# A row of numbers behind every gather of layers 1 and 2

## The chip, the cores and the metric

The kernel runs on one core of a Trainium2 chip. The metric is the device time of one execution in microseconds (us). Before the change three runs took 1017.23, 1017.79 and 1019.32 us; the median is 1017.79 us. The engines are TensorE (PE in the profile; PEld is its weight load), VectorE (DVE), ScalarE (ACT), GpSimd (POOL) and SyncE (SP), beside 16 DMA engines.

## The reference, cut to what matters

The reference puts four graph layers over a node matrix `x` of 2708 x 512 floats and one adjacency matrix `adj` of 2708 x 2708, which is sparse and has its largest degrees in the first rows. Each layer is wrapped as `x = layernorm(x + layer(x, adj))`.

```python
# layer 1
head = mask / maximum(sqrt(sum(mask * mask, -1)), EPS)   # mask = adj > 0
inc = adj + head
y = (inc @ x) / sum(inc, -1)
# layer 2
type_sum = adj @ x
attn_a = sigmoid(concat(type_sum, x) @ Wa.T + ba)         # attn_b likewise with Wb, bb
h = x @ W_sa
e = where(adj != 0, exp(-leaky_relu(s_left[:, None] + s_right[None, :], 0.01)), 0)
x_a = (e / (sum(e, 1) + 1e-5)) @ h
x_b = adj @ (x @ W_gcnb) + b_gcnb
y = sigmoid(attn_a * x_a + attn_b * x_b)
```

Layer 0 is a normalised `adj @ x` followed by a projection, and layer 3 multiplies the adjacency with the product of the signs of `x` and of a weight. Layers 1 and 2 are the ones that the change touches.

## The kernel before

**Blocks and tiles.** The 2708 rows are 22 blocks of up to 128 rows (`NB`, the last has 20 rows). Column block 0 of the adjacency is dense enough to be kept whole; for every other block `b` the kernel finds the nodes that have an edge into it, and packs their adjacency rows into `ROOM[b]` tiles of 128 nodes each (`packed[b]`, lists of node numbers in `index[b]`). `ROOM` falls from 9 to 4, and is 1 for the last block; over all blocks that makes 107 tiles. A tile that is used by only 64 of the block's rows is multiplied as a half tile (`HALVES`).

**A first stage** reads the adjacency, makes the lists, projects `x` for layer 0, and fetches the packed rows with one indirect DMA for each tile (`fetch`, L1011). Behind each of those fetches, for the groups in `RESTED` (L1008: all groups but the last three), GpSimd also fills a scratch tile `rest` of 128x384 floats with zeros (L1018).

**Gathers.** Each of the layers then gathers, for every one of its tiles, the feature rows of that tile's 128 nodes from a DRAM copy, with one indirect DMA that GpSimd issues: `gathered` (L582) for layers 0, 1 and 3, `gathered_2` (L1719) for layer 2. In layer 1 a row is 512 floats (256 KB a gather), in layer 2 it is 1026 floats, the features, their projection `h` and two scores (about 525 KB).

**Layer 1** (L1507 to L1615) goes over the blocks in the order 0, 1, 21, 2, 3, ... (`sequence`). For a block it issues all gathers (L1581 to L1583), lets DVE make the incidence tiles (`inc`, L1597, L1598), and PE adds the products of all tiles into one PSUM bank (`add_tile`, L1316). Between the blocks PE also transposes and projects the finished block before (`project1`, L1526 and L1533, with ACT copies at L1528 and L1539) and adds to block 0's sums for layer 2 (`grow2`, L1566 and L1567). The gathers have eight buffers: the pool `s_l1` has `bufs=8`. A gather can start when the tile eight places earlier has been multiplied.

**Layer 2** (L1621 to L1907) does the parts of a block in turn. For each part, `prepare` issues the gathers, and ACT and DVE make the attention weights: a score is added by ACT for each tile (L1489), DVE applies the slope (L1490), a mask (L1492, L1493), and ACT the exponential (L1494). `accumulate` then multiplies each tile twice, once with weights and once with the adjacency (L1744). Here the gathers have seven buffers. The layernorm of this layer has one small power operation on GpSimd for each block (L644), which sits in the same queue as the gathers.

**Order.** Each engine runs its instructions in one fixed order. In the first stage the text's order is forced (`in_order`); elsewhere the framework's scheduler chooses it at build time, from priorities in the order of the text and from its own model of durations and readiness. A dependency without a semaphore (`NoSync`) only constrains that order.

Of the kernel before, what the change touches and what calls it, by code (L numbers as in the profile page):

```python
# [19 lines left out]
P = 128  # L20
# [475 lines left out]
def sparse_layers(ctx, tc, x, adj, adj_t, w0_t, b0, w_sa, a_sa, w_gcnb, b_gcnb, wa, ba, wb, bb, w3_t,  # L496
# [11 lines left out]
    nc = tc.nc  # L508
# [7 lines left out]
    def rows(b: int) -> int:  # L516
        return min(P, N - b * P)

    def direct(b: int):

        return tuple(range(NB)) if b == 0 else DIRECT.get(b, ())
# [4 lines left out]
    const = ctx.enter_context(tc.tile_pool(name="s_const", bufs=1))  # L526
# [46 lines left out]
    dia_pos = const.tile([P, NB], F32, name="s_dia_pos")  # L573
    own0 = const.tile([P, NB], F32, name="s_own0")
    own1 = const.tile([P, NB], F32, name="s_own1")
    head0_row = const.tile([P, P], F32, name="s_head0_row")
    cols = const.tile([P, NB, EXTRA], F32, name="s_cols")

# [3 lines left out]
    def gathered(pool, dst_w: int, src, b: int, i: int, dtype=F32):  # L582
        t = pool.tile([P, dst_w], dtype, tag="xg", name=f"xg{b}_{i}")
        nc.gpsimd.indirect_dma_start(  # L584
            out=t, out_offset=None, in_=src[:, :],
            in_offset=bass.IndirectOffsetOnAxis(ap=index[b][:, i : i + 1], axis=0),
        )
        return t

    @contextmanager  # L590
    def in_order():
# [77 lines left out]
    with tc.tile_pool(name="s_pre", bufs=1) as pre:  # L669
# [36 lines left out]
        for d in (y_rows, x1_rows, x2_rows, xw_rows):  # L706
# [17 lines left out]
            channel_multiplier=-1,  # L724
# [5 lines left out]
            base=-1, channel_multiplier=-1,  # L730
# [5 lines left out]
            base=1 - P, channel_multiplier=1,  # L736
# [540 lines left out]
    def features(b: int, i: int, old0):  # L1277

        j = direct(b)[i]
        return f[j] if j else old0  # L1280
# [196 lines left out]
    def open_sums(b: int):  # L1477

        k = banks[0] % 2
        banks[0] += 1  # L1480
        state[b]["sums"] = [
            ps_acc.tile([P, D], F32, tag=f"{c}{k}", name=f"{c}{b}") for c in ("e", "a")
        ]

    def weights_of(e, mask, parts):

        for ev, _, sl, _, scores in parts:
            for i, score in enumerate(scores):
                nc.scalar.activation(ev[:, i, :], sl, AF.Identity, bias=score)  # L1489
        nc.vector.scalar_tensor_tensor(e, e, SLOPE, e, op0=ALU.mult, op1=ALU.max)  # L1490
        for _, mv, _, a, _ in parts:
            nc.vector.tensor_scalar(mv, a, 0.0, MASKED, op0=ALU.is_equal, op1=ALU.mult)  # L1492
        nc.vector.tensor_tensor(e, e, mask, op=ALU.add)  # L1493
        nc.scalar.activation(e, e, AF.Exp, scale=-1.0)  # L1494
# [12 lines left out]
    with tc.tile_pool(name="s_l1", bufs=8, reuse_waits="tile") as lp:  # L1507
        def gate_columns(dst, c: int, pool, tag: str):

            pv = pool.tile([P, D], F32, tag=tag, name=f"pv2_{c}")  # L1510
            nc.tensor.transpose(pv[:, : 2 * KC], vrows[:, c, :], ident[: 2 * KC, : 2 * KC])
            nc.vector.tensor_copy(
                dst.rearrange("p k t -> p t k"),
                pv[:, : 2 * KC].rearrange("p (t k) -> p t k", t=2),
            )

        gate_columns(wsa[:, :, D + 2 :], 0, ps_mm, "mm")
        H = D // 2
        hs = {}

        def project1(j: int):

            m = rows(j)
            pt = ps_mm.tile([P, KC, P], F32, tag="sum0", name=f"xt1p_{j}", bufs=1)
            for k in range(KC):
                nc.tensor.transpose(pt[:, k, :m], f[j][:m, k * P : (k + 1) * P], ident[:m, :m])  # L1526
            xt = lp.tile([P, KC, P], F32, tag="xt1", name=f"xt1_{j}", bufs=2)
            nc.scalar.copy(xt[:, :, :m], pt[:, :, :m])  # L1528
            p0 = ps_acc.tile([P, D], F32, tag="a1", name=f"h0_{j}")
            p1 = ps_acc.tile([P, D], F32, tag="e1", name=f"h1_{j}")  # L1530
            for ps, w in ((p0[:m, :H], wsa[:, :, :H]), (p1[:m, : H + EXTRA], wsa[:, :, H:])):
                for k in range(KC):
                    nc.tensor.matmul(  # L1533
                        ps, xt[:, k, :m], w[:, k, :], start=(k == 0), stop=(k == KC - 1)
                    )
            h = kept[j] if j < 2 else lp.tile(
                [P, D + EXTRA], F32, tag="h", name=f"h_{j}", bufs=4
            )
            nc.scalar.copy(h[:m, :H], p0[:m, :H])  # L1539
            nc.vector.tensor_copy(h[:m, H:], p1[:m, : H + EXTRA])  # L1540
            nc.sync.dma_start(x2_rows[j * P : j * P + m, D:], h[:m, : D + 2])
            nc.vector.tensor_copy(cols[:m, j, :], h[:m, D:])
            hs[j] = h

        grown2 = []

        def grow2(js):

            r, n, st = rows(js[0]), len(js), state[0]
            e = lp.tile([P, G2, P], F32, tag="e0", name=f"e0_{js[0]}", bufs=2)[:r, :n, :]  # L1550
            mask = lp.tile([P, G2, P], F32, tag="mask0", name=f"m0_{js[0]}", bufs=1)[:r, :n, :]
            a = packed[0][:r, js[0] : js[0] + n, :]
            weights_of(
                e, mask, [(e, mask, st["sl"][:r], a, [cols[:r, j, 0:1] for j in js])]
            )
            for i in range(n):
                if grown2 or i:
                    nc.vector.tensor_tensor(
                        st["esum"][:r], st["esum"][:r], e[:, i, :], op=ALU.add
                    )  # L1560
                else:
                    nc.vector.tensor_copy(st["esum"], e[:, i, :])
            for i, j in enumerate(js):
                at = dict(start=(not grown2), stop=(len(grown2) == NB - 1))
                se, sa = st["sums"]
                nc.tensor.matmul(se, e[:, i, :], hs.pop(j)[:r, :D], **at)  # L1566
                nc.tensor.matmul(sa, a[:, i, :], f[j][:r], **at)  # L1567
                grown2.append(j)

        G2 = 2  # L1570
        left = [(0, 1), (NB - 1,)] + [
            tuple(range(j, min(j + G2, NB - 1))) for j in range(2, NB - 1, G2)
        ]

        for at, b in enumerate(sequence):
            m = rows(b)
            if b:
                nd = len(direct(b))
                order_ = in_turns(b)
                src = {i: features(b, i, first[1]) for i in range(nd)}  # L1580
                for i in order_:  # L1581
                    if i >= nd:
                        src[i] = gathered(lp, D, x1_rows, b, i - nd)  # L1583
                ps = ps_mm.tile([P, D], F32, tag="mm", name=f"l1_{b}")
                inc_of = {}
                for i0, n, (r0, r1) in runs_of(b, 3):
                    a = packed[b][:, i0 : i0 + n, r0:r1]
                    half = r1 - r0 == HALF
                    inc = lp.tile(
                        [P, 3, HALF if half else P], F32, tag=f"inc{int(half)}",  # L1590
                        name=f"inc{b}_{i0}", bufs=4 if half else 3,
                    )
                    iv = inc[:, :n, : r1 - r0]
                    row = head_row[:, None, b * P + r0 : b * P + r1].to_broadcast(
                        [P, n, r1 - r0]
                    )
                    nc.vector.scalar_tensor_tensor(iv, a, 0.0, row, op0=ALU.is_gt, op1=ALU.mult)  # L1597
                    nc.vector.tensor_tensor(iv, iv, a, op=ALU.add)  # L1598
                    for i in range(n):
                        inc_of[i0 + i] = iv[:, i, :]  # L1600
                for i in order_:
                    add_tile(ps, b, i, inc_of[i], src[i][:, :D], order_)
            else:
                ps = sum1
            if left and left[0][-1] in sequence[: max(at - 2, 0)]:
                grow2(left.pop(0))
            finish1(b, ps)
            if at:
                project1(sequence[at - 1])
            if at == 1:  # L1610
                open_block(0, wp2, ps_mm, "mm")
                open_sums(0)
        project1(sequence[-1])
        for js in left:
            grow2(js)  # L1615
# [5 lines left out]
    with tc.tile_pool(name="s_l2o", bufs=1, reuse_waits="tile") as op, \  # L1621
# [97 lines left out]
        def gathered_2(b: int, t: int):  # L1719
            g = lp.tile([P, XW], F32, tag="xg", name=f"xg2_{b}_{t}", bufs=7)  # L1720
            nc.gpsimd.indirect_dma_start(  # L1721
                out=g, out_offset=None, in_=x2_rows[:, :],
                in_offset=bass.IndirectOffsetOnAxis(ap=index[b][:, t : t + 1], axis=0),
            )
            return g

        def accumulate(b: int, c: int):
# [402 lines left out]
```

## Time and profile before

The profile is of one execution, which was itself slower than the timed runs.

| what | value |
|---|---|
| timed runs, median | 1017.79 us |
| the profiled execution's own time | 1063.61 us |
| its span, first to last instruction | 1061.9 us |
| mean granted PE clock | 0.942 |
| PE busy | 893.4 us (84%) |
| DVE busy | 663.5 us (62%) |
| POOL busy | 569.7 us (54%) |
| ACT busy | 385.5 us (36%) |
| gathers of layer 1, L584 from `x_rows` | 107, 968 ns each |
| gathers of layer 2, L1721 from `x_rows` | 107, 993 ns each |
| layer 1 | about 382 to 622 us |
| layer 2 | about 622 to 934 us |

A line of groups in the profile names a line of the kernel, an engine, an operation and its tiles (output<-inputs), then the count, the busy time in us and the mean duration of one in ns, and then the idle time of the engine just ahead of it with what ended most of it. "remote" is a wait that ended with no instruction that the profile could name as its end; "issue" is a gap for which it shows no wait. The names leave buffer numbers out, so `x_rows` stands for layer 1's and layer 2's DRAM copies alike.

### The profile page before, as it was taken

Reading aid. Unit: us, or ns where it says so; the run is one execution under the profiler, and the core shown is the slowest. Engines: PE = TensorE matmul, PEld = TensorE weight load, DVE = VectorE, ACT = ScalarE, POOL = GpSimd, SP = SyncE. Lnnn points to the kernel's source line nnn. Section 1 sums busy time; section 2 is a strip of 40 time slices with the busy share of each in tenths; the row PEclk is TensorE's granted clock in tenths of the full one; section 3 lists DMA queues with packets and bytes.
Section 4 is the critical chain, followed back from the end, with each engine's and each line's share of the span. In section 5 each row is a group of like instructions: output and inputs, shape, how many; then the busy total and the mean of one; then the engine's idle time right before and its main releaser. Section 6 shows DMA issues by size and latency. Waiting matters only on the chain.

```text
span 1061.9 us, 13166 instructions
## 1 busy us (share of the span) xinstructions
PE 893.4 (84%) x3793; PEld 465.5 (44%) x3793; DVE 663.5 (62%) x2571; ACT 385.5 (36%) x821; POOL 569.7 (54%) x621
## 2 busy tenths in 40 slices
PE   1989996078788978899999999998889999689994
PEld 1545552022123324455455543443535555467772
DVE  4899998125566745345555346666758877646666
ACT  3566662000000013445344334333334333255554
POOL 1799998766666544555434034534434333057762
PEclk9899999589898988999999999999999999989996
DMA  9999984356776745666645266668677665299986
GB/s 265 349 321 322 336 263 144 82 171 209 231 210 207 227 139 145 184 209 189 208 144 168 95 233 216 238 223 288 205 230 230 200 195 201 80 269 311 321 233 214
DMA packets 96294, 231.16 MB, mean 218 GB/s; under 512 B 14204, under 2 KB 27884, under 8 KB 96212
## 3 DMA queue, kind: packets, MB, share of 16 engines
q0 software_dynamic: 46896, 139.22, 44.3%
q1 hardware_dynamic: 37368, 76.25, 20.9%
q10 hardware_dynamic: 11948, 14.76, 4.3%
q8 instruction: 32, 0.52, 0.2%
q14 instruction: 50, 0.41, 0.1%
HBM read 188.51 MB, written 31.71 MB: 207 GB/s over the span
## 4 chain that ended last, share of the span: by engine, by line
PE 52%; DVE 12%; DMA 11%; POOL 10%; another core or an unknown queue 6%; issue 6%; ACT 3%; ACTq 0%; POOLq 0%; SPq 0%; DVEq 0%
PE l L1316 14%; DMA xg<-x_rows,i 8%; PE h L1533 7%; POOL a L1013 6%; PE l L1999 4%; PE a L1744 4%; PE e L1744 4%; PE l L2038 3%; POOL s_rest L1018 3%; PE pg L1796 2%; PE pc L1796 2%; PE l L1371 2%; PE e L1566 1%; PE px L1857 1%
## 5 line engine op out<-in xcount | busy, mean ns | idle before, releaser
L1721 POOL DMA_INDIRECT xg<-x_rows,i x107 | 106.2, 993 | 170.3 <-PE a L1744 40.9
L584 POOL DMA_INDIRECT xg<-x_rows,i x107 | 103.6, 968 | 115.9 <-PE l L1316 73.1
L1013 POOL DMA_INDIRECT a<-in_adj_t_dram,row_at x107 | 115.8, 1082 | 46.6 <-DVE deg L773 21.4
L584 POOL DMA_INDIRECT xg<-y_rows,i x107 | 104.6, 978 | 52.6 <-issue 24.1
L1316 PE MATMUL l<-xg,a 128*64 128x512 f32 (+1 forms) x214 | 98.0, 652 | 27.5 <-DMA xg<-y_rows,i 26.9
L584 POOL DMA_INDIRECT xg<-xw_rows,i x76 | 79.6, 1048 | 38.6 <-issue 17.9
L1744 PE MATMUL a<-xg,a 128*64 128x512 f32 (+1 forms) x214 | 92.8, 603 | 4.5 <-DMA xg<-x_rows,i 4.5
L1744 PE MATMUL e<-xg,ae 128*64 128x512 f32 (+1 forms) x214 | 90.3, 603 | 2.7 <-ACT ae L1494 2.6
L1533 PE MATMUL h<-s_wsa,xt 128*128 128x256 f32 (+3 forms) x352 | 83.8, 392 | 6.9 <-ACT xt L1528 6.8
L1045 PE MATMUL y<-s_w,xt 128*128 128x512 f32 (+1 forms) x176 | 86.9, 640 | 0.0
L1316 PE MATMUL l<-xg,inc 128*64 128x512 f32 (+1 forms) x214 | 79.4, 613 | 3.6 <-DMA xg<-x_rows,i 3.1
L1533 PEld LDWEIGHTS h<-s_wsa,xt 128*128 128x128 f32 (+1 forms) x352 | 65.0, 189 | 33.5 <-ACT xt L1528 15.6
L1489 ACT ACTIVATE ae<-sl,xg 128x64 f32<-128x64 f32 (+1 forms) x107 | 37.5, 359 | 99.1 <-DMA xg<-x_rows,i 88.6
L765 ACT ACTIVATE unused<-arow 128x1408 uint8<-128x1408 f32 (+3 forms) x44 | 58.3, 1325 | 3.8 <-DMA x_rows<-s_zero 3.0
L1316 PEld LDWEIGHTS l<-xg,a 128*64 128x64 f32 (+1 forms) x214 | 25.1, 160 | 78.4 <-DMA xg<-y_rows,i 41.5
L1424 DVE SCALAR_TENSOR_TENSOR t<-l,s_dinv,f 128x512 f32<-128x512 f32 (+1 forms) x21 | 15.6, 744 | 64.6 <-remote 44.7
L1999 PE MATMUL l<-ws,pw 128*128 128x512 f32 (+1 forms) x210 | 51.5, 400 | 3.9 <-DVE pw L1927 3.9
L613 ACT ACTIVATE rsqs<-mv 128x1 f32<-128x1 f32 (+2 forms) x56 | 11.3, 202 | 112.1 <-DVE mv L642 45.8
L1540 DVE COPY h<-h 128x260 f32<-128x260 f32 (+1 forms) x20 | 8.6, 428 | 66.3 <-PE h L1533 47.5
L1045 PEld LDWEIGHTS y<-s_w,xt 128*128 128x128 f32 (+1 forms) x176 | 33.8, 203 | 36.5 <-issue 36.4
L1490 DVE SCALAR_TENSOR_TENSOR ae<-ae 128x128 f32<-128x128 f32 (+5 forms) x56 | 19.2, 343 | 45.8 <-ACT ae L1489 45.1
L1796 PE MATMUL pg<-s_wg,pt 128*128 128x256 f32 (+1 forms) x176 | 44.7, 392 | 2.8 <-ACT pt L1784 2.8
(302 smaller groups left out, 1887.2 us busy)
## 6 DMA issues: line engine op xcount, KB each, us to landing
arow<-in_adj_dram SPq DMA_DIRECT2D x21, 704.0 KB
arow<-in_adj_dram SPq DMA_DIRECT2D x21, 650.0 KB
x_rows<-f SPq DMA_DIRECT2D x41, 256.0 KB
aw<-in_adj_t_dram SPq DMA_DIRECT2D x21, 320.0 KB
f<-in_x_dram SPq DMA_DIRECT2D x20, 256.0 KB
y_rows<-yt ACTq DMA_DIRECT2D x20, 256.0 KB
out_dram<-f SPq DMA_DIRECT2D x20, 256.0 KB
x_rows<-h SPq DMA_DIRECT2D x19, 257.0 KB
```

The source lines that it names most:

```text
L584: nc.gpsimd.indirect_dma_start(out=t, out_offset=None, in_=src[:, :], in_offset=bass.IndirectOffsetOnAxis(ap=index[b][:, i : i + 1], axis=0),)
L765: nc.scalar.activation(unused[:m, : ar.shape[1]], ar, AF.Copy, accum_out=row_sums[:m, b, h : h + 1])
L1013: nc.gpsimd.indirect_dma_start(out=packed[b][:, t + len(direct(b)), :], out_offset=None, in_=adj_t, in_offset=bass.IndirectOffsetOnAxis(ap ...
L1018: nc.gpsimd.memset(rest, 0.0)
L1045: nc.tensor.matmul(ps[:m], xt[:, k, :m], w0[:, k, :], start=(k == 0), stop=(k == KC - 1))
L1316: nc.tensor.matmul(ps[r0:r1], weights, moving, start=(i == order[0]), stop=all(span(b, j) != (r0, r1) for j in order[order.index(i) + 1 :] ...
L1489: nc.scalar.activation(ev[:, i, :], sl, AF.Identity, bias=score)
L1533: nc.tensor.matmul(ps, xt[:, k, :m], w[:, k, :], start=(k == 0), stop=(k == KC - 1))
L1721: nc.gpsimd.indirect_dma_start(out=g, out_offset=None, in_=x2_rows[:, :], in_offset=bass.IndirectOffsetOnAxis(ap=index[b][:, t : t + 1], a ...
L1744: nc.tensor.matmul(ps[r0:r1], weights, moving, start=(i == order[0]), stop=all(span(b, k) != (r0, r1) for k in order[order.index(i) + 1 :] ...
L1796: nc.tensor.matmul(ps, pt[:, k, :m], w[:, k, :], start=(k == 0), stop=(k == KC - 1))
L1999: nc.tensor.matmul(whole[b], p[:r, h, b * P : (b + 1) * P], g[:r, :], start=(j == 0 and h == 0), stop=(j == NB - 1 and h == 1),)
```

## The change

A scratch tile `numbers` of 128x448 16-bit integers is added to the constants. A new helper finds the last instruction that was traced for GpSimd, which is the gather, writes the numbers 0 to 447 into every row of the scratch tile with an `iota` on GpSimd, and ties the iota behind the gather in the build-time order. It is called behind each of the 107 gathers of layer 1 and each of the 107 of layer 2. Nothing reads the scratch tile.

```diff
+    numbers = const.tile([P, 448], mybir.dt.int16, name="s_numbers")
...
+    def last_on_pool():
+        return next(
+            i for i in reversed(nc.cur_bb.bb.instructions) if i.engine == mybir.EngineType.Pool
+        )
+
+    def rest_behind_gather():
+        gather = last_on_pool()
+        nc.gpsimd.iota(numbers, pattern=[[1, 448]], base=0, channel_multiplier=0)
+        tc.add_manual_dep(
+            last_on_pool(), gather.name,
+            mybir.DependencyInfo(mybir.DependencyClass.NoSync, mybir.DependencyReason.DATA),
+            reason="rest_behind_gather",
+        )
...
                 for i in order_:
                     if i >= nd:
                         src[i] = gathered(lp, D, x1_rows, b, i - nd)
+                        rest_behind_gather()
...
                 in_offset=bass.IndirectOffsetOnAxis(ap=index[b][:, t : t + 1], axis=0),
             )
+            rest_behind_gather()
             return g
```

## The prediction

> **What bounds the kernel now.** I read the busy time by stage first (columns: stage in us, its length, busy us and count of PE, PEld, DVE, ACT, POOL, granted PE clock, DMA share, GB/s). The third row is layer 1, the fourth layer 2.
>
> ```profile
> 0.00:177.00 177.00, 141.61 (x1022) 78.25 (x1022) 150.38 (x660) 98.37 (x175) 136.97 (x178) 0.96 0.88 286
> 177.00:382.00 205.00, 141.77 (x425) 43.48 (x424) 105.47 (x462) 11.48 (x43) 130.01 (x132) 0.86 0.63 188
> 382.00:622.00 240.00, 224.21 (x774) 118.53 (x775) 115.00 (x461) 98.02 (x170) 103.87 (x108) 0.96 0.57 168
> 622.00:934.00 312.00, 279.92 (x1152) 142.56 (x1150) 213.68 (x765) 112.75 (x308) 119.27 (x129) 0.99 0.64 211
> ```
>
> PE carries both layers: it idles 15.8 us in layer 1 and 32.1 us in layer 2. POOL is free for 136 and 193 us there, so 107 more instructions in each have room on average; what matters is where they fall. Second, the groups and waits of the engines concerned.
>
> ```profile
> L1721 POOL DMA_INDIRECT xg<-x_rows,i x107 | 106.2, 993 | 170.3 <-PE a L1744 40.9 <-ACT ae L1489 36.5 <-PE e L1744 34.7
> L584 POOL DMA_INDIRECT xg<-x_rows,i x107 | 103.6, 968 | 115.9 <-PE l L1316 73.1 <-issue 22.6 <-DVE inc L1597 15.5
> L1018 POOL MEMSET s_rest<- 128x384 f32 x82 | 44.0, 537 | 0.1
> L743 POOL IOTA s_slot<- 128x1152 int16 x1 | 1.1, 1089 | 0.0
> L750 POOL IOTA s_start_i<- 128x22 int32 x1 | 0.1, 137 | 0.0
> ```
>
> ```profile
> ACT ae L1489 <- DMA xg<-x_rows,i: 88.6, 61, 3.9
> ```
>
> GpSimd mostly waits for PE to free a buffer; in layer 2 ACT in turn waits for gathers to land, 61 times, 88.6 us in all. Third, the timeline of POOL: two rested fetches of the first stage, then the unrested run that opens layer 1.
>
> ```profile
> 150.43 1.00 POOL L1013 DMA_INDIRECT a<-in_adj_t_dram,row_at  x1 [0.16 <-issue]
> 151.43 0.43 POOL L1018 MEMSET s_rest<- 128x384 f32 x1
> 152.03 0.94 POOL L1013 DMA_INDIRECT a<-in_adj_t_dram,row_at  x1 [0.16 <-issue]
> ...
> 390.06 0.95 POOL L584 DMA_INDIRECT xg<-x_rows,i  x1 [0.30 <-issue]
> 391.32 0.95 POOL L584 DMA_INDIRECT xg<-x_rows,i  x1 [0.30 <-issue]
> ```
>
> Unrested gathers follow each other every 1.25 us (0.95 + 0.30 gap), rested ones about every 1.55 to 1.6 (0.95 + 0.43 + 0.16). Fourth, the timeline at the end of that run of 17 gathers, and the clock by stage around it.
>
> ```profile
> 400.22 2.88 PE L1533 MATMUL h<-s_wsa,xt 128*128 128x256 f32 x12
> 406.11 0.37 ACT L1539 COPY s_h<-h 128x256 f32<-128x256 f32 x1 [10.44 <-remote]
> 407.73 0.45 PE L1469 MATMUL slp<-s_ident,s_cols 128*128 128x128 f32 x1 [4.62 <-DVE rs L633]
> ```
>
> ```profile
> 402.00:406.00 4.00, 1.11 (x6) 0.61 (x4) 2.12 (x6) 0.00 (x0) 1.37 (x2) 1.00 0.66 174
> 406.00:413.00 7.00, 5.27 (x10) 2.23 (x11) 4.19 (x17) 2.29 (x6) 0.94 (x1) 0.51 0.35 117
> 438.00:443.00 5.00, 3.89 (x12) 3.12 (x13) 0.00 (x0) 2.39 (x4) 1.89 (x2) 0.72 0.53 153
> ```
>
> The matmuls of `h` show as ended by 403.1, yet ACT's copy, which waits only for them, starts at 406.11: PE's completion was told 3.0 us late, shortly after the gathers paused. PE then waits 4.62 us for what follows from that copy, and runs its next 7 us at clock 0.51. The same recurs after the run from 418 to 437: ACT's L1528 idles 1.96 us for "remote" until 438.47, then PE idles 3.02 us until 439.11. In the trace's record of PE's semaphore, lags of 2 us and more occur in layer 0, layer 1 and layer 3, all during unrested runs of nine or more gathers; none occurs in the rested first stage (at most 1.1 us, at a higher DMA share), nor in layer 2, whose runs have at most nine and mostly four.
>
> **What the Trainium skill says.** SBUF — State Buffer, § Who interferes with whom: VectorE in its two-port mode and a GpSimd instruction lock each other out for a whole instruction; a GpSimd one that only writes does not disturb two-input VectorE work. The trace agrees in that the rest takes 432 ns at least but up to 1079. Perfetto Trace Analysis, § GPSIMD Engine Instruction: time GpSimd by start-to-start spacing; I do so. The same page, § Tensor Engine Instruction: a matmul's end is an estimate. So the 3.0 us lag could be PE still working; but at clock 1.00 twelve matmuls begun 0.22 us apart leave no such backlog. TensorE: Matmul & The Clock Gate, § What's actually happening: about 3.4 us of idling halve the clock; 0.51 after 406 agrees.
>
> **The change part by part.** Nothing is removed.
>
> *The scratch tile* costs nothing by itself; 896 bytes a partition only move addresses.
>
> *Price of one iota.* From the two rows, (1089 - 137) / (1152 - 22) = 0.84 ns an element, so 137 + 426 x 0.84 = 0.50 us (the 22-wide one is 32-bit; if width counted, 448/1152 x 1089 = 0.42). As with the fill, the gap behind it should be 0.16. Back to back, a gather then takes 0.95 + 0.50 + 0.16 = 1.61 us instead of 1.25: +0.36. POOL gets 214 x 0.50 = 107 us of work into 329 us of idle time. Against an idle queue the iota runs while GpSimd waits for a buffer, and costs 0.
>
> *Layer 1, lateness.* Adding 0.36 for each gather in a run, and taking idle time off, the opening run is late by 2.8 us at its ninth gather and 5.3 at its sixteenth. The ninth was used 6.65 us after issue; the first three were used as soon as 3.6 to 4.8 us after theirs. So its margin is 1.8 to 3.0: PE loses 0 to 1.0 us. The sixteenth had 17.9 us: hidden by block 1's projection and block 21. In the run from 418 the gathers at 423.62 and 425.04 have 5.4 and 5.05 us, and come 1.4 and 1.8 late: another 0 to 1.5. Every later one has over 7.4 us except one at 459.06 (5.8, 1.1 late). Together 0 to 2.5; I take 0.8. If PE's other work did not cover it, the opening would pass on all 2.8.
>
> *Layer 1, relief.* If rests stop the late completions as they seem to in the first stage, this returns 3.0 us at 403 and 2.0 at 438, and the half clock behind them: 7 x 0.49 = 3.4 and 5 x 0.28 = 1.4. That is 9.8 us at most, and 0 at least. I take half, 4.9, because the run is only thinned from 1.25 to 1.61 and a part of the lag may belong to the profiled execution.
>
> *Layer 2, gathers.* ACT's adds that wait for landings start at 689.33, 691.34, 693.07 and 694.93, so landings are 1.7 to 2.0 us apart: the 525 KB transfer, not the issue, spaces them. 1.61 is still below. The delay is hidden by the transfer of the gather before, 0; if not, it is the rival below.
>
> *Layer 2, queue.* Behind each iota sit the next gather and the power operations (22 x about 0.58 us). In five places (659.19, 765.53, 779.54, 812.01, 822.60) the power operation directly follows a gather and would start up to 0.5 us later, with DVE's L654 behind it and the gather after it: at most 5 x 0.5 = 2.5, mostly under PE's other products. *VectorE lock.* Iotas fill 53 us of layer 2's 312, 17%. Some 170 two-port operations (78 of L1492, the rest L654, L1844 and the like, eight a block) would be blocked 0.25 us on average in 17% of cases: 7 us of DVE, which is 68% busy; at most a third, 2.4, reaches PE. For both together I take 0.7 of 0 to 4.9.
>
> *Order.* The scheduler sees a longer POOL and may shift instructions on other engines. The trace can't price that; I bound it at -3 to +3 and take 0.
>
> Sum against the profiled execution: -4.9 + 0.8 + 0.7 = -3.4, so 1063.6 becomes 1060.2. That execution lies 45.8 us above the median; I carry the difference over: 1017.8 - 3.4 = 1014.4.
>
> **The rivals.** *Slower: the issue decides layer 2's landings.* Place: ACT's L1489. If transfers alone would land closer than 1.61 us, each of 61 waits grows by 0.36: 22 us for ACT, of which PE's idle share (32.1 of 88.6, 36%) is 7.9. With no relief and layer 1's 0.8: 1026.5; with a third of the waits affected, 1021.2. Against it: the spacing of 1.7 to 2.0. For it: 61 waits with no margin. *No difference.* The late completions stay, or exist only under the profiler, and everything else is hidden, or relief and costs cancel: 1017 to 1019. For it: POOL's idle time; against it: exact balance is a narrow target. *Full relief*: -9.8 + 1.5 = 1009.5. *It doesn't do what it says* (iotas gathered elsewhere in the queue): the tie and the text's order speak against it; time as before.
>
> **How the numbers follow.** A measurement can tell about 0.2%, 2 us, from no change. Relief beats cost: 0.43 (partial 0.31, full 0.12), own range 1008 to 1015.7. No difference: 0.19. Slower: 0.38, for the lateness, the lock and a worse order each have no cover that I can prove. Range 1007 to 1024: 0.08 lie below (full relief with a lucky order), 0.10 above.
>
> **What would show it.** 107 iotas in each layer at about 0.5 us; runs spaced 1.6 us; ACT's L1539 starting close behind PE's last `h` in block 0, no "remote" waits near 406 and 438, clock near 1 there; ACT's wait for landings in layer 2 still near 89 us. I am wrong if those waits stay or move, if ACT's wait grows by ten us or more, or if layer 1 shortens in the profile but not in the timed runs.

## The result, and the profile after

The changed kernel took 1027.97 us (median of 7 runs, 1023.91 to 1032.29) against 1019.32 us for the kernel before in the same runs: a ratio of 1.0081, 95% interval 1.0054 to 1.0107. It is slower by about 8 us; the forecast was 1014.4 us.

The groups of the changed kernel in the page (busy us, mean ns | idle us ahead of it), and its GpSimd in the run that opens layer 1 (start, length, gap ahead):

```profile
L1737 POOL DMA_INDIRECT xg<-x_rows,i x107 | 105.3, 984 | 107.5 <-PE a L1761 34.8
L585 POOL DMA_INDIRECT xg<-x_rows,i x107 | 103.7, 969 | 53.0 <-PE l L1331 24.3
L598 POOL IOTA s_numbers<- 128x448 int16 x214 | 111.4, 521 | 2.1
```

```profile
371.75 0.95 POOL L585 DMA_INDIRECT xg<-x_rows,i  x1 [0.17 <-issue]
372.71 0.52 POOL L598 IOTA s_numbers<- 128x448 int16 x1
373.39 0.95 POOL L585 DMA_INDIRECT xg<-x_rows,i  x1 [0.17 <-issue]
```

The rows do what was foreseen of them: 0.52 us each (forecast 0.50), gathers in a run 1.64 us apart (forecast 1.61). The idle time ahead of the gathers is 53.0 and 107.5 us in layers 1 and 2, against 98.6 and 168.1 us in the second profile of the kernel before (below). (Lines of the changed kernel stand 15 to 17 later: L1316 is L1331, L1489 is L1504, L1721 is L1737, L1744 is L1761.)

By layer, counted here and below from a layer's first gather to the next layer's, the changed kernel shows (length, busy us of PE, PEld, DVE, ACT, POOL, clock, DMA share, GB/s):

```profile
363.20:595.20 232.00, 227.50 (x774) 117.86 (x775) 117.68 (x461) 98.35 (x170) 159.06 (x214) 0.98 0.59 174
595.20:911.20 316.00, 281.47 (x1136) 142.19 (x1152) 222.27 (x766) 113.75 (x308) 174.93 (x236) 0.98 0.64 209
```

Against the profile that the forecast read (239.6 us counted the same way), layer 1 is *shorter* by 7.6 us; so is layer 0, which the change does not touch: its gathers ran from 210.4 to 348.5, and from 210.0 to 366.9 before. The whole span is 31 us shorter, while the timed runs are 8 us longer. The two profiles cannot be subtracted.

### The profile page after: what moved, and what is told of

Read it like the earlier page. It is cut to its first block, busy times and chain, and to the rows that moved or that the text cites. A ratio compares the mean times of both kernels' runs of the same rounds, so it can differ in the third digit from the quotient of the medians.

```text
span 1030.6 us, 13347 instructions
## 1 busy us (share of the span) xinstructions
PE 898.0 (87%) x3775; PEld 463.8 (45%) x3793; DVE 676.8 (66%) x2571; ACT 387.1 (38%) x821; POOL 680.6 (66%) x835
## 3 DMA queue, kind: packets, MB, share of 16 engines
q0 software_dynamic: 46896, 139.22, 45.8%
## 4 chain that ended last, share of the span: by engine, by line
PE 48%; DMA 19%; DVE 13%; POOL 11%; issue 6%; ACT 2%; ACTq 0%; POOLq 0%; SPq 0%; DVEq 0%
PE l L1331 9%; DMA xg<-y_rows,i 9%; DMA xg<-x_rows,i 8%; PE h L1548 6%; PE l L2016 5%; PE a L1761 4%; PE e L1761 4%; PE l L2055 4%; POOL xg L585 3%; PE y L1060 3%; POOL a L1028 3%; POOL s_numbers L598 2%; DVE s_mask L843 2%; PE pc L1813 2%; PE pg L1813 2%
## 5 line engine op out<-in xcount | busy, mean ns | idle before, releaser
L1737 POOL DMA_INDIRECT xg<-x_rows,i x107 | 105.3, 984 | 107.5 <-PE a L1761 34.8
L1028 POOL DMA_INDIRECT a<-in_adj_t_dram,row_at x107 | 112.2, 1048 | 45.8 <-DVE deg L788 20.8
L1331 PE MATMUL l<-xg,a 128*64 128x512 f32 (+1 forms) x214 | 101.3, 625 | 30.1 <-DMA xg<-y_rows,i 28.5
L598 POOL IOTA s_numbers<- 128x448 int16 x214 | 111.4, 521 | 2.1
L585 POOL DMA_INDIRECT xg<-xw_rows,i x76 | 77.3, 1017 | 34.2 <-issue 13.2
L1761 PE MATMUL a<-xg,a 128*64 128x512 f32 (+1 forms) x214 | 92.3, 613 | 5.6 <-DMA xg<-x_rows,i 5.6
L1761 PE MATMUL e<-xg,ae 128*64 128x512 f32 (+1 forms) x214 | 88.5, 613 | 5.8 <-ACT ae L1509 5.8
L1331 PE MATMUL l<-xg,inc 128*64 128x512 f32 (+1 forms) x214 | 83.7, 608 | 2.8 <-DMA xg<-x_rows,i 2.7
L1548 PEld LDWEIGHTS h<-s_wsa,xt 128*128 128x128 f32 (+1 forms) x352 | 64.6, 188 | 28.8 <-ACT xt L1543 10.7
L1504 ACT ACTIVATE ae<-sl,xg 128x64 f32<-128x64 f32 (+1 forms) x107 | 38.0, 359 | 80.7 <-DMA xg<-x_rows,i 72.0
L1331 PEld LDWEIGHTS l<-xg,a 128*64 128x64 f32 (+1 forms) x214 | 24.7, 152 | 86.1 <-DMA xg<-y_rows,i 61.7
L659 POOL TENSOR_TENSOR rs<-mv,s_neg_half 128x1 f32<-128x1 f32 (+1 forms) x22 | 14.0, 635 | 58.5 <-DVE mv L657 56.2
L1033 POOL MEMSET s_rest<- 128x384 f32 x82 | 48.9, 596 | 0.1
```

The costliest lines, as they stand in the source:

```text
L585: nc.gpsimd.indirect_dma_start(out=t, out_offset=None, in_=src[:, :], in_offset=bass.IndirectOffsetOnAxis(ap=index[b][:, i : i + 1], axis=0),)
L598: nc.gpsimd.iota(numbers, pattern=[[1, 448]], base=0, channel_multiplier=0)
L1028: nc.gpsimd.indirect_dma_start(out=packed[b][:, t + len(direct(b)), :], out_offset=None, in_=adj_t, in_offset=bass.IndirectOffsetOnAxis(ap ...
L1033: nc.gpsimd.memset(rest, 0.0)
L1331: nc.tensor.matmul(ps[r0:r1], weights, moving, start=(i == order[0]), stop=all(span(b, j) != (r0, r1) for j in order[order.index(i) + 1 :] ...
L1548: nc.tensor.matmul(ps, xt[:, k, :m], w[:, k, :], start=(k == 0), stop=(k == KC - 1))
```

## The experiments

Two devices recur. The scheduler is shown one width of the number row while it orders the program, and the width is changed afterwards (`set_rests`), so that order and time are separated. With the number rows left out, rows of 4 leave the order of the kernel before on every engine, as far as the names and shapes in the traces tell; rows of 448 give a new one in the opening blocks of layer 1 and in layer 2, mostly blocks 1 to 12. And the gathers of one block can be followed by all its number rows together.

A row need not stand directly behind its gather. The tie only puts it somewhere behind: at 11 of the 107 gathers of layer 2 (14 in the changed kernel) the layernorm's power operation stands between the gather and its row.

The five sessions of experiments were of two kinds. In three of them the kernel before took 1016.35, 1016.75 and 1016.45 us, in two 1068.66 and 1067.8 us. The expectations call this a difference of chips. One chip was used in a session of each kind, so the chip alone does not make it; I say "quick" and "long" sessions.

### The kernel before, profiled again

No edit.

> The kernel before, unchanged, profiled a second time. Theory 'the lag belonged to one execution': the 45.8 us that the first profile lay above the timed runs are gone (a span of about 1020 us), no PE completion near the gather runs of layer 1 arrives late, the first layer (which the change does not touch) is again near 138 us of gathers as after the change, not 157, and layer 1 is shorter than after's 232 us, near 226. Rival 'unrested gathers delay completions': layer 1 again carries some 10 us of waits with the releaser 'remote' or half clock, and lies near 240 us.

It took 1015.18 us with a span of 1013.5 us. Its layers 1 and 2:

```profile
362.80:585.40 222.60, 218.15 (x774) 115.84 (x775) 115.01 (x461) 98.12 (x170) 103.58 (x108) 0.99 0.60 182
585.40:895.40 310.00, 279.02 (x1136) 142.66 (x1153) 214.39 (x766) 112.97 (x309) 119.23 (x130) 0.99 0.64 213
```

The lag is gone: layer 0's gathers end at 347.3, no wait in the whole trace ends with "remote", and block 0's copy of `h` starts at 380.10, 17.3 us after the layer's first gather, not 24.0:

```profile
378.93 2.88 PE L1533 MATMUL h<-s_wsa,xt 128*128 128x256 f32 x12
380.10 0.37 ACT L1539 COPY s_h<-h 128x256 f32<-128x256 f32 x1 [5.51 <-PE h L1533]
```

It starts 1.2 us after the twelve matmuls begin, because L1539 copies the first half of `h` only and needs just the first four of the twelve. So in the first profile, where they began at 400.22, the copy at 406.11 was 4.7 us late, not 3.0. That profile was of a long session's kind; in layer 1 it had, among others,

```profile
ACT s_h L1539 <- remote: 10.4, 1, 10.4
ACT xt L1528 <- remote: 2.0, 1, 2.0
```

Seen against this profile, the changed kernel is 9.4 us longer in layer 1 and 6.0 in layer 2 (6.4 us, and 4.5 and 5.7, in two later executions of it). Such differences scatter by some us: the stages ahead of layer 1, which no edit touches, take 356.6 to 363.2 us in the eleven quick executions. None of the eleven has a wait for "remote": there was nothing to relieve in the kind of run that was timed.

### Time on GpSimd, or the new order?

```diff
-        nc.gpsimd.iota(numbers, pattern=[[1, 448]], base=0, channel_multiplier=0)
+        nc.gpsimd.iota(numbers[:, :4], pattern=[[1, 4]], base=0, channel_multiplier=0)
```

This is "short" (rows of 4, old order). "Old order, full" adds `set_rests(nc, 448)` behind the scheduler. "New order, short" is the changed kernel with `set_rests(nc, 4)`. "New order, none" is the changed kernel with the rows taken out behind the scheduler.

> The same 214 number rows of 448 as in the changed kernel, but every engine's order of instructions is that of the kernel before (the rests were 4 wide while the order was made, and were widened to 448 afterwards). Theory 'time on POOL' (the half microsecond behind each gather makes rows land later and slows VectorE beside it): the whole loss, 6 to 10 us over before. Rival 'order' (the scheduler, shown a dearer instruction, placed other work differently): within 2 us of before.

> The order of the changed kernel, with the number rows only 4 wide (made 448 wide for the ordering, narrowed afterwards). Theory 'time on POOL': within 2 us of before, since the rests take a tenth of the time. Rival 'order': 6 to 10 us over before, as the changed kernel.

> Number rows 4 wide from the start, and the order of the kernel before: 214 more instructions on POOL, nearly no time (an estimate of 0.1 us each, from the 0.5 us of 448 numbers). Both theories: 0 to 1 us over before. If the instruction itself costs (its issue between two gathers), 3 us or more over before, and then part of e2 is that and not the width.

> The order of the changed kernel without any number row, a second time. On a chip of 1016 us: the order's gain in layer 2 alone, 0.993 to 0.997. On a chip of 1065 us: as the first time, 0.980 to 0.990.

| quick sessions, ratio to before (95%) | old order | new order |
|---|---|---|
| no row | 1 | 0.9954 (0.9937 to 0.9971) |
| rows of 4 | 1.0037 (1.0021 to 1.0053) | 0.9982 (0.9965 to 1.0000) |
| rows of 448 | 1.0183 (1.0154 to 1.0212) | 1.0081 (1.0054 to 1.0107) |

The last cell is the result above; two more sessions gave it 1.0073 and 1.0103 (below). Full rows in the old order cost 1.8% (18.6 us), twice what the change shows; the new order, a by-product, gives about 1% of that back, and without any row it is faster than the kernel before (1012.59 us against 1016.75). "Order" as the rival had it (the order itself is the loss) has fallen. Rows of 4 already cost 0.37%, 3.8 us, so about 15 of the 18.6 us belong to the rows' width.

Where the full rows cost, in the old order: first layers 1 and 2 of "old order, full" by length, then its groups in layer 2, below them the same groups of the kernel before profiled again, and at last layer 2 of "short" and its first group.

```profile
356.60:587.00 230.40, 222.18 (x773) 116.51 (x774) 118.38 (x463) 98.23 (x170) 158.93 (x214) 0.99 0.60 176
587.00:911.40 324.40, 286.63 (x1136) 144.69 (x1152) 220.21 (x766) 113.31 (x308) 174.03 (x236) 0.96 0.63 203
```

```profile
L1761 PE MATMUL a<-xg,a 128*64 128x512 f32 (+1 forms) x214 | 96.0, 631 | 8.9 <-DMA xg<-x_rows,i 8.9
L1761 PE MATMUL e<-xg,ae 128*64 128x512 f32 (+1 forms) x214 | 94.2, 641 | 2.1 <-ACT ae L1509 2.0
L1507 DVE TENSOR_SCALAR mask<-a 128x128 f32<-128x128 f32 (+2 forms) x77 | 22.1, 337 | 0.7
```

```profile
L1744 PE MATMUL a<-xg,a 128*64 128x512 f32 (+1 forms) x214 | 92.7, 602 | 3.3 <-DMA xg<-x_rows,i 3.2
L1744 PE MATMUL e<-xg,ae 128*64 128x512 f32 (+1 forms) x214 | 90.3, 603 | 2.7 <-ACT ae L1494 2.6
L1492 DVE TENSOR_SCALAR mask<-a 128x128 f32<-128x128 f32 (+2 forms) x77 | 16.2, 233 | 0.7
```

```profile
584.00:903.30 319.30, 282.27 (x1135) 144.26 (x1152) 212.25 (x765) 113.35 (x309) 136.60 (x237) 0.97 0.63 207
```

```profile
L1761 PE MATMUL a<-xg,a 128*64 128x512 f32 (+1 forms) x214 | 94.0, 609 | 4.6 <-DMA xg<-x_rows,i 4.5
```

Layer 2 is 14.4 us longer with full rows, but 9.3 of this is there with rows of 4. PE's own wait for rows to land is 3.2 us without rows, 4.5 with rows of 4 and 8.9 with full ones; 8.9 came again in the quick run with full rows in layer 2 alone (below). So what the width adds in layer 2 lies mainly in the landings. The two groups of matmuls that use those rows are also 7.2 us longer in this execution (602 to 631 and 603 to 641 ns each, granted clock 0.99 to 0.96); in that other run they took 620 and 604 ns, so this part did not recur in full. VectorE's mask is slower, 233 to 337 ns, and ScalarE waits 5 us longer for the product behind it (30.3 to 35.6), but PE's wait behind the exponential, which comes next, is not longer (2.6 to 2.0). No run here separates that slowing from the landings in layer 2.

In layer 1 (7.8 us longer) the same matmuls show:

```profile
L1331 PE MATMUL l<-xg,inc 128*64 128x512 f32 (+1 forms) x214 | 82.5, 609 | 5.6 <-DMA xg<-x_rows,i 5.6
```

```profile
L1316 PE MATMUL l<-xg,inc 128*64 128x512 f32 (+1 forms) x214 | 78.5, 608 | 2.8 <-DMA xg<-x_rows,i 2.8
```

2.8 us more of waiting for rows, and 4.0 us more of busy time for equally long matmuls: 214 x 0.608 is 130 us of matmuls in 78.5 us of busy time, so most of them overlap another by the profile, which models their ends; with full rows behind the gathers fewer do. With rows of 4 both stand as before (2.8 and 78.9 us; layer 1 takes 224.0 us), so in layer 1 it is the width.

### One layer at a time

`set_rests(nc, 448, 4)` and `(4, 448)`: full rows in layer 1 alone or in layer 2 alone, old order. The first pair fell into a long session, the second into a quick one.

> Order of the kernel before; number rows of 448 in layer 1, of 4 in layer 2. Theory 'rows land late in both layers' (by the profiles, layer 1 took 222.6 us before and 230.4 with full rests in the old order): about 7 us over the kernel with 4 wide rows in both, so ratio about 1.010. Rival 'layer 2 alone pays, as the stage whose ScalarE waits on landings': ratio about 1.004, as with 4 wide rows.

> Order of the kernel before; number rows of 4 in layer 1, of 448 in layer 2. Theory 'rows land late in both layers': about 7 us over the kernel with 4 wide rows in both, ratio about 1.011, and the two layers' losses add up to the 15 us between 4 wide and full. Rival 'layer 2 alone pays': ratio 1.018, the whole loss.

> Order of before, number rows of 448 in layer 1, of 4 in layer 2, a second time. On a chip of 1016 us: both layers pay, 7 us over the kernel with 4 wide rows, 1.010. On a chip of 1065 us: as the first time, 0.993 to 0.999.

> Order of before, number rows of 4 in layer 1, of 448 in layer 2, a second time. On a chip of 1016 us: 5 to 8 us over the kernel with 4 wide rows in both, 1.009 to 1.012. On a chip of 1065 us: as the first time, 1.000 to 1.006.

| ratio to before (95%) | quick | long |
|---|---|---|
| full in layer 1, 4 in layer 2 | 1.0090 (1.0056 to 1.0124) | 0.9963 (0.9935 to 0.9991) |
| 4 in layer 1, full in layer 2 | 1.0089 (1.0056 to 1.0123) | 1.0031 (1.0006 to 1.0056) |

In quick sessions each layer pays about 5 us over rows of 4. That is 10.7 us together, of the 14.8 between rows of 4 and full ones; the two were measured in different sessions, and each interval is about 3.4 us to either side. In a long session full rows in layer 1 make the kernel *faster*. It was run again there, beside rows of 224 in both layers:

> Beside it, for the pair: full number rows in layer 1 one by one, 1.009 on a chip of 1016 us, 0.996 on one of 1065 us.

> Number rows of 224 in both layers, order of before (4 wide: 1.0037, 448: 1.0183 on a chip of 1016 us). If the loss grows with the time of the row from the first (every gather that is late is waited for): half way, 1.011. If slack covers the first part of it (landings spaced wider than the issue, as the prediction has it for layer 2): near the 4 wide rows, 1.005.

0.9958 (0.9935 to 0.9982), and 0.9976 (0.9956 to 0.9997) for rows of 224. Their profiles show where. Without a row in the old order, layer 1 took 239.6 us in the first profile and 236.7 us in the other kernel of that kind (the one with the power moved, below). Here is that one, then rows of 4 in layer 1 (full in layer 2), and at last full rows, all of the long kind:

```profile
386.70:623.40 236.70, 220.78 (x774) 116.97 (x775) 114.61 (x461) 98.03 (x170) 103.45 (x108) 0.97 0.57 171
```

```profile
383.20:611.40 228.20, 219.62 (x773) 115.76 (x774) 114.69 (x461) 98.30 (x170) 121.95 (x214) 0.99 0.59 177
```

```profile
383.40:614.80 231.40, 224.50 (x773) 116.58 (x774) 117.88 (x461) 98.23 (x170) 161.72 (x215) 0.99 0.59 175
```

The same wait of 10.4 us for "remote" at the copy of `h` stands in both executions without rows. With full rows layer 1 has no wait for "remote" at all, in either run (231.4 and 230.2 us); with rows of 4 and 224 shorter ones remain (3.1 and 4.7 us the longest), and yet layer 1 takes no longer (228.2 and 230.1 us). With full rows in the old order, layer 1 takes 230 to 232 us in both kinds of session; what differs most is the kernel before, 222.6 or 239.6 us.

By these profiles, then, most of the relief does not need the width. By the traces block 0's copy starts 0.04 us after the last matmul that it reads in all eleven quick executions, and also in all six long ones with number rows, whether the rows are 4, 224 or 448 wide, one by one or behind a block's last gather. In the three long ones without rows it is later than that, by 4.7 and 5.1 us in the old order and by 2.5 us in the new one. Rows of 4 only move the gathers of a run from 1.25 to 1.27 us apart; why their presence is enough for the copy is open. The times leave room for a part of the width in the rest: from quick to long sessions the ratio falls by 1.3% with full rows in layer 1 and by 0.6% with the two widths the other way round.

What half the width costs in a quick session, and so whether slack covers a first part of it, was not measured.

### The order without rows, in a long session

> The order of the changed kernel, with the number rows taken out after the ordering (the counts on the semaphore that they raised lowered to match). If the order alone is a gain that the 4 wide rows half hid (0.9982 with them, and 4 wide rows cost 0.37% in the old order): 0.994 to 0.995 of before, 5 us faster. If the 4 wide rows cost nothing in the new order: 0.998.

0.9849 (0.9800 to 0.9898); layer 1 took 229.7 us and has no wait for "remote", though block 0's copy is still 2.5 us late; layer 2 took 307.7 us. So the new order relieves layer 1 there too, by one profile.

### All number rows of a block behind its last gather

In layer 1, old order, 4 wide in layer 2 (`held` is emptied at a block's last gather):

```diff
+                new.append(ins[g])
+                held.append(ins[r])
```

> As the run with full rows in layer 1 alone, but all number rows of a block of layer 1 stand behind that block's last gather, so the gathers of a block go out back to back (1.25 us, not 1.6); the time on POOL is the same. Theory 'lateness of the gathers': at least half of layer 1's loss comes back. Rival 'POOL beside VectorE' (the number rows slow VectorE's two-operand passes wherever they stand): same time as with full rows in layer 1, within 2 us.

> Full number rows in layer 1 alone (4 wide in layer 2), order of before, each block's number rows behind its last gather. On a chip of 1016 us, where the same rows one by one gave 1.009: theory 'lateness of the gathers' expects at least half of layer 1's 5 us back, 1.004 to 1.0065; rival 'POOL beside VectorE' 1.008 to 1.010. On a chip of 1065 us, where it was within 0.3% of before, again 0.997 to 1.003.

> Full number rows in layer 1 alone behind each block's last gather, order of before, 4 wide rows in layer 2. On a chip of 1016 us, not measured yet: theory 'lateness of the gathers' 1.004 to 1.0065, rival 'POOL beside VectorE' 1.008 to 1.010. On a chip of 1065 us: 1.000 to 1.006 a third time.

Long sessions: 0.9995 (0.9966 to 1.0025) and 1.0041 (1.0020 to 1.0062), the second beside 0.9958 for the rows one by one. Quick session: 1.0124 (1.0084 to 1.0165), where one by one gave 1.0090 in another session (1.0056 to 1.0124). Layer 1 takes 237.3 to 237.5 us in all three, 5 to 7 more than one by one. So nothing comes back, against the first theory. That the time is not the same either, against the rival, rests on the profiles and on the second long session, where the two kernels were timed side by side (1070.57 and 1064.42 us); the quick intervals overlap. In the quick sessions, layer 1 one by one and then behind the last gather:

```profile
L1331 PE MATMUL l<-xg,inc 128*64 128x512 f32 (+1 forms) x214 | 83.4, 618 | 7.2 <-DMA xg<-x_rows,i 6.3 <-DVE inc L1613 0.8
```

```profile
L1331 PE MATMUL l<-xg,inc 128*64 128x512 f32 (+1 forms) x214 | 83.9, 617 | 11.2 <-DMA xg<-x_rows,i 6.1 <-DVE inc L1613 1.9 <-DVE rsqs L639 1.8
```

A likely reading, argued and not shown: one by one, many rows run while GpSimd would wait for a buffer anyway; together they stand in front of the next block's gathers with all their time. As POOL's time is equal and the place changes the result, VectorE's slowing is not the whole of layer 1's loss.

### GpSimd's part of the new order alone

The kernel before, with the power operation of ten blocks of layer 2 one gather earlier (block 5 two), as in the changed kernel.

> The kernel before, no number row, every order as before except POOL's: in ten blocks of layer 2 the power of the layernorm stands one gather earlier (block 5 two), as in the changed kernel. If that is the order's gain: 0.994 to 0.997 as with the whole new order. If the gain is ScalarE's and TensorE's new order: 0.999 to 1.001.

1.0152 (1.0117 to 1.0188), slower, in a long session. Layer 2 takes 335.3 us (312.8 in the first profile of before), and GpSimd's queue stands in front of the power for what VectorE has not made yet, 74.4 us instead of 42.3 there:

```profile
POOL rs L644 <- DVE mv L642: 74.4, 14, 10.3
```

So the gain is not GpSimd's part alone; neither expected outcome came. In "new order, none" of the quick session ScalarE's adds wait 66.9 us for landings (90.6 in the kernel before); the new order puts other work of ScalarE ahead of several of them. Which of the moves on PE, DVE and ACT carries the gain was not isolated.

### The changed kernel again

> The changed kernel again. Theory 'two chips': on a chip where before takes about 1016 us and no completion is late, the change costs (1.006 to 1.011); on a chip where before takes about 1065 us and PE's completions come late in the profile (as in the profile that the prediction was made from), layer 1 gains 7 to 11 us, the new order of layer 2 some 5, the number rows of layer 2 cost 10: 0.990 to 0.998. Rival 'one price on every chip': 1.006 to 1.011 on both.

> The changed kernel, unaltered. On a chip of 1016 us: 1.007 to 1.008 a third time. On a chip of 1065 us, where it has not been timed: theory 'the relief is there and the loss too, they nearly cancel' expects the new order without rows (0.985) plus the two rows' net effects there (layer 1 about -0.4%, layer 2 about +0.7%): 0.985 to 0.995; rival 'one price on every chip': 1.007.

1.0073 (1.0050 to 1.0095) and 1.0103 (1.0068 to 1.0139), both in quick sessions. In a long one it has not been timed.

## Why the prediction was wrong

- **The step that failed first is "Layer 1, relief" (-4.9 us), together with the 45.8 us "carried over".** In executions like the profiled one the rows do end late completions, and shorten layer 1 from 239.6 (236.7) to 231.4 (230.2) us, so -4.9 was even small. But the timed runs were of another kind, in which no completion is late and layer 1 takes 222.6 us. An execution 4.5% above the median was taken as the median plus a constant, though the effect to be cured was part of those 45.8 us. The forecast named the case (late completions that exist only under the profiler) and gave it too little.
- **The mechanism of the relief is not shown even in the long kind.** The forecast took half of it because the run is thinned only from 1.25 to 1.61 us; rows of 4, at 1.27 us, shorten layer 1 as much by their one profile (228.2 us). Its reading was short too: the copy was 4.7 us late, not 3.0, since it needs only the first half of those products. And the record of PE's semaphore, from which it told stages with lags from stages without, has only 685 updates for 825 instructions that raise it (826 in the second profile), so a missing entry can pass for a late one; what stands are the late starts.
- **"Layer 1, lateness" (+0.8, bound 2.5) was undersized.** Measured: 7.8 to 9.3 us by the profiles in the old order (222.6 to 230.4 and 231.9), 5 us by the times of full rows over rows of 4. The working counted when a row's first use would wait (2.8 us more); it left out the other 4.0 us, where by the profile matmuls overlap less.
- **"Layer 2, gathers" (0) was wrong**, and the rival "the issue decides layer 2's landings" right in direction. PE's wait for landings grew from 4.5 us with rows of 4 to 8.9 with full ones. That the transfer of the gather before hides the delay is not borne out: in layer 2 the median from issue to landing is 6.3 and 5.8 us in two runs with rows of 4, and 5.0 and 5.8 in two with full ones. The rival's 7.9 us was PE's share of ACT's longer waits; but ACT's wait, 90.6 us without rows, was already 97.4 with rows of 4 and 99.1 with full ones, so the width barely moved it.
- **A cost of the row itself, whatever its width, was not in the sum:** 3.8 us with rows of 4.
- **"Layer 2, queue" and "VectorE lock" (0.7)**: in all five places that the forecast named, the power operation came to stand ahead of the row and not behind it, so what the row stands in front of there is the next gather. VectorE's busy time in layer 2 rose by 5.8 us (214.4 to 220.2), nearly all of it the mask, near the 7 us worked out; that it hardly reached PE fits the path through the mask (2.6 to 2.0 us).
- **"Order" (0, bounded at -3 to +3) was undersized and fell outside its bound.** It is worth -0.46% without rows, 4.7 us, and about -1% with them. It hid half of the loss.
- **Price and spacing** of the number row were right (0.52 for 0.50 us, 1.64 for 1.61 us). What would show the forecast wrong, "layer 1 shortens in the profile but not in the timed runs", is what came.

The forecast was -3.4 us and the result +8.3. Of these 11.7 us the missing relief is 4.9. The rest is two errors of opposite sign: the rows cost about 18 us in the timed kind of run, where 1.5 were forecast, and the order returned about 10, where none was. That the result lies only 4 us above the range, 1007 to 1024, is thus partly luck. The range left out the rival's full case, 1026.5, and no case let both layers pay.

## What to carry to other kernels

When a profiled execution lies several per cent from the timed runs, find where that time sits before using it: an effect found there can be part of the difference, and then must not be forecast for the timed runs. Work in a queue that is idle for more than half of a layer can still cost time, if what stands behind it is used soon; judge it by the margins of its users, and take the landings and their users' overlap together. Before a wait is put down to spacing, try the same instructions at almost no length: here rows of 4 removed the late start at the copy as well as full ones did. When an edit lets a scheduler reorder, separate time from order by showing it one size and running another: here they had opposite signs, and the order without the edit was the best kernel (0.9954 of before).

## What was not expected of the hardware

- The same kernel took 1016 us in some sessions and 1068 in others. In the long kind, a wait of 10.4 us that ends with "remote" recurs at the same place of layer 1 in the old order without rows, the untouched layer 0 takes 157 to 161 us of gathers (136 to 138 in the quick kind), and fewer updates of PE's semaphore are in the trace (666 to 711 for 825 or 832 instructions in the nine long executions; 823 to 834 in the eleven quick ones). What makes the kinds is open.
- A row of 4 numbers takes 0.15 us, and a gather with it and its gap 1.27 us instead of 1.25; still 214 of them cost 0.37%, by the profiles in layer 2 (319.3 to 320.0 us in three quick executions with rows of 4 there, against 310.0 in the one profile without). In two of the three ScalarE waits 97.4 and 97.7 us for landings, against 90.6. What causes it is open.
